# A graph layer whose edge rows go through memory: sends of the next chunk moved ahead of the first fetch, and one block's lists ahead of the first table's stores

## The chip, the cores and the metric

The kernel runs on one core of a Trainium2 chip. The metric is device time in microseconds (us) for one launch, the median of several runs. Engines are named as in the profile: PE (matrix), DVE (vector), ACT (scalar), POOL (GpSimd), SP (the queue from which most plain DMAs leave).

## The reference

```python
h = relu(layernorm(x))                       # x: 12500 x 64
# 212500 edges, sorted by dst; ew: one weight per edge
e = silu(concat(h[row], h[col], ew) @ eW1 + eb1)      # 129 -> 128
e = silu(e @ eW2 + eb2)                               # 128 -> 128
agg = segment_sum(e, row, num_segments=12500)
out = x + silu(concat(h, agg) @ nW1 + nb1) @ nW2 + nb2
```

Here `row` is `src` and `col` is `dst`; the edges come sorted by `dst`.

## The kernel before, in words

The first product is split: A = h @ eW1[:64] is looked up by `src`, B = h @ eW1[64:128] by `dst`. A is kept in memory as table `ta` (three bf16 parts per value), B as table `tb`. Since the edges come sorted by `dst`, the B row of an edge lies in a small window of `tb`; the rows of A and the sums go by `src`, which is in random order. So each edge's partial row is sent through memory to a place that belongs to the bucket of its source (100 buckets of 125 nodes), and read back bucket by bucket.

**Send side.** The edges come in 208 blocks of 1024. For block s:

- `load` reads two lists (`bc`, `bb`: positions in the window and buckets, L265 and L267) for one block further on, and two windows of 48 rows of B for block s itself (L277). All go out from SP's queue. The windows of the first `EARLY` blocks come from a small table `tb0` (the first 2048 nodes) that is ready early; later ones from `tb`.
- `count` makes, on DVE, the selection matrix `pick` (L302), the bucket mask `oh` (L303), its running count (L306) and `own` (L314), and has SP load the edge weights into `pick` (`weights`, L288).
- `send` takes ranks (L333) and the B rows times selection (L341) on PE, copies them to `qs` on ACT (L348, L357), forms addresses `to` on DVE (L353), and sends 128 edges at a time with an indirect DMA from POOL (L362), eight per block. `qs` has eight buffers (of four sends each), `to` four.

A block's sending is cut into `PIECES` = 3 pieces. Blocks are grouped into 11 chunks: 8 blocks in chunk 0, 20 in each later one, each with its own table `q`. `send_all(c)` yields the pieces of a chunk; on its way it also issues the zero fills of the next chunk's `q` (L100, ACT's queue), and it runs the count of one block ahead.

**Receive side.** A batch is four buckets of one chunk, 25 batches in each chunk. `fetch` loads its rows from `q` and its rows of `ta` (L407, L412, both on SP), four batches ahead (`NQ`). A step handles 512 rows: local indices turned (`lr`, L430), one-hot (`oneT`, L435), first layer (`pt`, L444 and L451, activated at L455), second layer (L477, L483, L487), sum by node (L464, L497), added to `aggT` (L506, L508). A batch has one step in chunk 0 and two in later chunks, 525 steps in all. In the last chunk `nodes` follows each batch and writes the output.

**Order.** PE, DVE, ACT and SP run in the order in which the program lists their instructions. The list is written by hand: `turn` gives the order of the parts of neighbouring steps, with four places (`None`, "hooks") per step, at which pieces of the next chunk and parts of `feed` are put in. `feed` is everything that makes `ta`, `tb` and the scaled bucket addresses of the later chunks (`normed`, `products`, `checks`). `marks` gives how many pieces must be out by which hook: all pieces of chunk c by the hook at which the first batch of c is fetched. Between two marks they are spread evenly: 60 pieces in 92 hooks while chunk 0 is received, 60 in 188 or 200 later.

Before the main loop stand the lists: `destinations` and `sources` write the table `rows` (L622, L640), `first_rows` makes `tb0` (stores at L557), then come block 0's scaling and loads, all eight blocks of chunk 0 with four parts of `feed` at each piece, and the first four fetches.

Of the kernel before, what the change touches and what calls it, by code (L numbers as in the profile page):

```python
# [46 lines left out]
G = 4  # L47
# [12 lines left out]
def tile_gnn(ctx: ExitStack, tc: tile.TileContext, x, src, dst, ew, eW1, eb1, eW2, eb2, nW1, nb1, nW2, nb2, out):  # L60
# [18 lines left out]
    chunks = []  # L79
# [25 lines left out]
            dma(to[part], of[part])  # L105

    CH = 12
    NE, EARLY = 16, 24
    x_rows = x.rearrange("(l b) d -> l b d", b=NB)

    ident = const.tile([P, P], F32, name="ident")
# [74 lines left out]
    bkE = const.tile([P, 2 * TB, NP], F32, name="bkE")  # L186
# [4 lines left out]
    for win in wins:  # L191
        nc.vector.memset(win, 0.0)
        for a in range(2):
            for i, row in enumerate((w1d, eb1b)):
                at = a * HB + WL + i
# [43 lines left out]
    with ExitStack() as work:  # L239
# [14 lines left out]
        blk = {}  # L254
        nblocks = -(-E // BLK)
        chunk_of = [c for c, ch in enumerate(chunks) for _ in range(2 * (ch[1] - ch[0]))][:nblocks]

        def load(s, ahead=0):

            if s + ahead < nblocks:  # L260
                p, g = (s + ahead) // 2, (s + ahead) % 2
                r = rows[p, g]
                bc = ld.tile([P, HALF], BF16, name="bc")
                of = bass.AP(tensor=r.tensor, offset=r.offset, ap=[[HALF, 2], [0, HB], [1, HALF]])
                nc.sync.dma_start(bc, of)  # L265
                bb = ld.tile([P, BLK], BF16, name="bb")
                nc.sync.dma_start(bb[:112], bass.AP(tensor=r.tensor, offset=r.offset + BLK, ap=[[0, 112], [1, BLK]]))  # L267
                blk[s + ahead] = [bc, bb]
            if 0 <= s < nblocks:
                p, g = s // 2, s % 2  # L270
                win = wins[s % NW]
                table, end = (tb0, NE * P) if s < EARLY else (tb, N)
                assert s < EARLY or len(done_b) == NB // G
                for a in range(2):
                    h = 2 * g + a
                    at = nc.sync.value_load(base_i[:, h, p : p + 1], min_val=0, max_val=end - WL)
                    nc.sync.dma_start(win[a * HB : a * HB + WL, :], table[bass.ds(at, WL), :])  # L277
                pick = ld.tile([P, HALF], F32, name="pick")
                blk[s] += [win, pick]
# [93 lines left out]
        def send_all(c):  # L373

            mine = [s for s in range(nblocks) if chunk_of[s] == c]
            zeros_left = list(fill(c + 1, nc.scalar, 7)) if c + 1 < len(chunks) else []
            each = -(-len(zeros_left) // len(mine))
            for s in mine:
                load(s + 2, 1)
                for f in zeros_left[:each]:  # L380
                    f()
                del zeros_left[:each]

                for i, _ in enumerate(itertools.zip_longest(count(s + 1), send(s))):
                    pending[c] -= i == PIECES - 1
                    yield
# [4 lines left out]
        PIECES = 1 + TB // G  # L391
        pending = [chunk_of.count(c) for c in range(len(chunks))]
# [125 lines left out]
        hooks = sum(1 for s in turn if s is None)  # L518
# [20 lines left out]
        def turned(xs, g):  # L539

            ht = mm.tile([P, G // 2, P], F32, name="ht", tag="mm")
            for i in range(G // 2):
                nc.tensor.transpose(
                    ht[:, i, :], xs[:, g + 2 * i : g + 2 * i + 2, :].rearrange("p j d -> p (j d)"), ident
                )
            hr = fp.tile([P, G // 2, P], F32, name="hr")
            nc.scalar.copy(hr, ht)
            return hr

        def first_rows(g):  # L550

            hr = turned(x0, g)
            yield
            got = fp.tile([P, G, H], F32, name="got")
            product(1, hr, mm, "mm", got)
            yield
            nc.sync.dma_start(tb0.rearrange("(p j) f -> p j f", j=NE)[:, g : g + G, :], got)  # L557
            yield
# [36 lines left out]
        def turns(todo, width):  # L595

            todo, doing = [x if type(x) is tuple else (None, x) for x in todo], []
            while todo or doing:
                if todo and len(doing) < width and (todo[0][0] is None or todo[0][0] in ready):
                    doing.append(todo.pop(0)[1])  # L600
                for d in list(doing):
                    if next(d, 0) == 0:
                        doing.remove(d)
                    else:
                        yield
# [37 lines left out]
        def by_edges(of, to):  # L643

            for k0 in range(0, 2 * TB, 4):
                tr = mm.tile([P, 4, NP], F32, name="tr", tag="mm")
                for k in range(4):
                    nc.tensor.transpose(tr[:, k, :], of[:, (k0 + k) * P : (k0 + k + 1) * P], ident[:NP, :NP])
                if to is locE:
                    nc.scalar.add(to[:, k0 : k0 + 4, :], tr, 1.0)  # L650
                else:
                    nc.scalar.copy(to[:, k0 : k0 + 4, :], tr)
                yield

        def scale(c):
            p0, p1, cap, _, _ = chunks[c]
            v = bkE[:, :, p0:p1]

            q4 = lp.tile([P, 2 * TB, p1 - p0], F32, name="q4", tag=f"q4{c > 0}")
            nc.vector.tensor_scalar(q4, v, 0.5 - G / 2, 1.0 / G, op0=OP.add, op1=OP.mult)  # L660
            nc.vector.tensor_scalar(q4, q4, float(3 * 2**22), None, op0=OP.add)
            nc.vector.tensor_scalar(q4, q4, -float(3 * 2**22), None, op0=OP.add)
            nc.vector.scalar_tensor_tensor(v, q4, float(cap * P * G - G), v, op0=OP.mult, op1=OP.add)
# [36 lines left out]
        with tc.tile_pool(name="lists", bufs=1, side="right") as lp:  # L700
            x0 = lp.tile([P, NE, D], F32, name="x0")
            nc.sync.dma_start(x0, x[: NE * P, :].rearrange("(p j) d -> p j d", j=NE))
            srcR = lp.tile([NP, PAIR], I32, name="srcR")
            dstR = lp.tile([NP, PAIR], I32, name="dstR")
            f, sf, t = (lp.tile([NP, PAIR], F32, name=n) for n in ("f", "sf", "t"))
            fv = f.rearrange("p (g e) -> p g e", e=HALF)
            lo = lp.tile([NP, 4], F32, name="lo")
            rowsS = lp.tile([NP, 2, 2, BLK], BF16, name="rowsS")
            nc.vector.memset(srcR[96:NP, LAST:], N)
            vec = lambda v, lo_, n, m: bass.AP(tensor=v.tensor, offset=v.offset + lo_, ap=[[m, n], [1, m]])  # L710
            for to, v, queue in ((dstR, dst, nc.scalar), (srcR, src, nc.sync)):
                for p0, p1 in ((0, 96), (96, NP - 1)):
                    queue.dma_start(to[p0:p1, :], vec(v, p0 * PAIR, p1 - p0, PAIR))
                queue.dma_start(to[NP - 1 : NP, :LAST], vec(v, (NP - 1) * PAIR, 1, LAST))
            nc.scalar.dma_start(dstR[NP - 1 : NP, LAST:], vec(dst, E - PAD, 1, PAD))
            zero_fills = list(fill(0, nc.scalar, 7))
            zero_fills.pop(0)()
            steps_ = [norm(x0, NE), destinations(), sources()]
            for _ in turns(steps_, 3):
                if zero_fills:  # L720
                    zero_fills.pop(0)()
            for _ in turns([by_edges(sf, bkE)] + [first_rows(g) for g in range(0, NE, G)], 3):
                pass
            scale(0)
            load(-1, 1)
            load(0, 1)
            load(1, 1)
            for _ in by_edges(t, locE):
                pass
            for _ in count(0):  # L730
                pass
            feed = itertools.chain(checks(), turns(groups(), 3))
            for _ in send_all(0):
                for _ in range(4):
                    next(feed, None)
# [8 lines left out]
            nc.scalar.copy(b2f, p2)  # L744
        ld2 = work.enter_context(tc.tile_pool(name="ld2", bufs=NQ))
        ndp = []
        for i in range(NQ):
            fetch(i)


        first = -3
        marks, total = [(0, 0)], 0
        for c in range(1, len(chunks)):
            start = c * (NB // G) - NQ
            by = sum(x[2] for x in batches[: start + 1]) - 2
            total += PIECES * pending[c]
            marks.append((hooks * (by - first), total))
        pieces = itertools.chain.from_iterable(send_all(c) for c in range(1, len(chunks)))
        at = done = 0
        for k in range(first, len(steps) + 2):  # L760
            for s in turn:
                if s is None:
# [16 lines left out]
                else:  # L779
                    f, ahead = s  # L780
# [8 lines left out]
    with tc.tile_pool(name="fl", bufs=1) as fl, tc.tile_pool(name="flp", bufs=1, space=PSUM) as flp:  # L789
        fp = flp.tile([1, P], F32, name="fp")  # L790
        s = fl.tile([P, 1], F32, name="s")
# [141 lines left out]
```

## Time and profile before

| | us |
|---|---|
| median of 3 runs (2700.62 to 2704.18) | 2703.32 |
| the profiled execution | 2702.45 |
| its span | 2700.7 |
| busy: PE / DVE / ACT / POOL | 2188.2 / 1874.6 / 1251.1 / 1818.5 |
| mean granted PE clock | 0.907 |

Busy times are those of one profiled execution and overlap each other. A group's row in the profile gives its busy time, the mean duration of one instruction in ns, and the idle time of its engine just before it with what ended most of that. A wait is put down to the one event that came last. The issue of a DMA takes its queue's time only for the issue; the transfer runs on without the queue.

### The profile page before, as it was taken

How to read it: one execution, taken by the hardware profiler on the slowest of the kernel's cores; microseconds unless marked ns; L12 is line 12 of the kernel's file. 1: busy time of each engine (PE TensorE's matmuls, PEld its weight loads, DVE VectorE, ACT ScalarE, POOL GpSimd, SP SyncE). 2: the span in 40 equal slices, each digit the busy share in tenths (PEclk: the TensorE clock that was granted, in tenths of full speed). 3: DMA queues.
4: the chain of work that ended last, by engine and by line, in shares of the span. 5: the costliest groups of instructions: out<-in, count | busy, mean ns of one | idle time of the engine just before them, and what ended most of it. 6: DMA issues, size and time to landing. Idle time of an engine off the chain costs nothing.

```text
span 2700.7 us, 59194 instructions
## 1 busy us (share of the span) xinstructions
PE 2188.2 (81%) x21814; PEld 2043.3 (76%) x21814; DVE 1874.6 (69%) x2634; ACT 1251.1 (46%) x2689; POOL 1818.5 (67%) x1728
## 2 busy tenths in 40 slices
PE   2436674898699599699879969959959987997997
PEld 1326574897699599599779869959958986996996
DVE  4736683796588488588768858848857885883443
ACT  2325551454355255355445535525535544553443
POOL 2546787777777777777777777777777777773000
PEclk9757786998899799799989989979989998998999
DMA  8668675876776777686787777767767755764441
GB/s 201 190 186 243 202 246 163 260 234 196 231 234 229 213 248 236 203 251 231 212 256 230 237 218 233 238 205 253 231 202 250 240 183 198 234 199 158 158 164 52
DMA packets 257969, 577.18 MB, mean 214 GB/s; under 512 B 51201, under 2 KB 110579, under 8 KB 257468
## 3 DMA queue, kind: packets, MB, share of 16 engines
q1 hardware_dynamic: 185096, 384.91, 44.3%
q0 software_dynamic: 54144, 123.04, 12.6%
q10 hardware_dynamic: 18434, 65.37, 10.5%
q8 instruction: 175, 2.87, 0.4%
q14 instruction: 120, 0.98, 0.1%
HBM read 361.44 MB, written 211.67 MB: 212 GB/s over the span
## 4 chain that ended last, share of the span: by engine, by line
PE 63%; DMA 13%; issue 6%; POOL 5%; DVE 2%; ACT 1%; SPq 0%; DVEq 0%; POOLq 0%; ACTq 0%
PE p L483 15%; PE seg L497 15%; PE pt L451 11%; DMA q<-qs,to 8%; PE pt L444 8%; PE qp L341 7%; POOL q L362 5%; PE lr L430 4%; DMA pick<-in_edge_weight_dram 3%; PE misc L333 1%; DMA bb<-rows 1%; PE z L216 1%; PE o L225 1%; DVE oneT L435 1%; PE z L219 1%
## 5 line engine op out<-in xcount | busy, mean ns | idle before, releaser
L362 POOL DMA_INDIRECT q<-qs,to x1661 | 1780.4, 1072 | 632.2 <-issue 445.6
L455 ACT ACTIVATE e<-pt 128x512 f32<-128x512 f32 x525 | 313.9, 598 | 778.0 <-PE pt L451 765.1
L483 PE MATMUL p<-w,e 128*128 128x128 f32 x4200 | 588.2, 284 | 2.2 <-ACT p L477 2.2
L497 PE MATMUL seg<-one,e 128*128 128x125 f32 x4200 | 576.8, 281 | 8.9 <-DVE aggT L506 5.7
L483 PEld LDWEIGHTS p<-w,e 128*128 128x128 f32 x4200 | 529.5, 198 | 27.5 <-issue 10.4
L497 PEld LDWEIGHTS seg<-one,e 128*128 128x128 f32 x4200 | 524.8, 196 | 11.2 <-ACT p L477 4.1
L435 DVE TENSOR_SCALAR oneT<-lr,part 125x512 bf16<-125x512 f32 x525 | 392.6, 748 | 197.5 <-PE lr L430 194.6
L306 DVE TENSOR_TENSOR_SCAN run<-oh,run,misc 100x1024 f32<-100x1024 f16 x197 | 461.1, 2341 | 1.0 <-PE misc L333 0.7
L451 PE MATMUL pt<-oneT,a 125*128 125x256 bf16 (+1 forms) x3300 | 444.6, 274 | 0.0
L341 PE MATMUL qp<-win,pick 50*128 50x128 f32 x3322 | 264.6, 300 | 205.0 <-DMA pick<-in_edge_weight_dram 119.9
L348 ACT COPY qs<-qp 128x512 f32<-128x512 f32 x416 | 224.7, 588 | 444.3 <-PE qp L341 312.0
L341 PEld LDWEIGHTS qp<-win,pick 50*128 50x128 f32 x3322 | 224.1, 202 | 237.8 <-issue 208.2
L444 PE MATMUL pt<-ident,qt 128*128 128x128 f32 x2100 | 332.8, 282 | 68.8 <-DVE oneT L435 68.8
L508 DVE TENSOR_TENSOR aggT<-aggT,seg 128x500 f32<-128x500 f32 x250 | 168.3, 673 | 315.7 <-PE seg L497 313.3
L464 DVE TENSOR_TENSOR one<-nodes,qt 128x500 f32<-128x500 f32 x525 | 353.4, 673 | 0.5 <-PE seg L497 0.5
L451 PEld LDWEIGHTS <-a 125*128 125x128 bf16 x3300 | 320.5, 100 | 34.5
L487 ACT ACTIVATE e<-p 128x512 f32<-128x512 f32 x525 | 314.6, 599 | 12.3 <-PE p L483 11.6
L477 ACT COPY p<-b2f 128x512 f32<-128x512 f32 x525 | 312.3, 595 | 0.1
L444 PEld LDWEIGHTS pt<-ident,qt 128*128 128x128 f32 x2100 | 228.4, 145 | 74.9 <-DVE oneT L435 72.9
L430 PE MATMUL lr<-identb,qt 128*125 128x128 bf16 x2100 | 215.1, 226 | 63.1 <-DMA qt<-q 63.0
L314 DVE TENSOR_TENSOR own<-run,oh 100x1024 f16<-100x1024 f32 x208 | 253.7, 1220 | 0.0
L430 PEld LDWEIGHTS <-qt 128*125 128x125 bf16 x2100 | 187.8, 140 | 75.6 <-DMA qt<-q 63.7
(122 smaller groups left out, 1094.5 us busy)
## 6 DMA issues: line engine op xcount, KB each, us to landing
qt<-q SPq DMA_DIRECT2D x250, 576.0 KB
a<-ta SPq DMA_DIRECT2D x275, 384.0 KB
q<-zeros ACTq DMA_DIRECT2D x30, 1638.0 KB
bb<-rows SPq DMA_DIRECT2D x208, 224.0 KB
bc<-rows SPq DMA_DIRECT2D x208, 128.0 KB
q<-qs,to POOLq DMA_INDIRECT x1661
win<-tb SPq DMA_DIRECT2D x416, 24.0 KB
ta<-parts SPq DMA_DIRECT2D x25, 384.0 KB
```

The costliest lines, as they stand in the source:

```text
L306: nc.vector.tensor_tensor_scan(run, oh, nil.to_broadcast([NB, BLK]), carry.get(c, -1.0), op0=OP.add, op1=OP.add)
L341: nc.tensor.matmul(qps[a][:, t, :], pick[half, t * P : (t + 1) * P], win[half, :], start=True, stop=True)
L362: i = nc.gpsimd.indirect_dma_start(out=q[:], out_offset=bass.IndirectOffsetOnAxis(ap=to[:k, t : t + 1], axis=0), in_=qs[:k, t - t0, :], in ...
L430: nc.tensor.matmul(lr[:L, t, :], loc[:, at : at + 1].to_broadcast([P, L]), identb, start=True, stop=True)
L435: nc.vector.tensor_scalar(oneT, st[k].pop("lr")[:L], part1[:L, :], None, op0=OP.is_equal)
L444: nc.tensor.matmul(pt[:, t, :], qt[:, j, :H], ident, is_transpose=True, start=t == 0, stop=False, skip_group_check=True)
L451: nc.tensor.matmul(pt[:, cols, :], a3[:L, b, i, :], oneT[:, cols, :], start=False, stop=i == 2, skip_group_check=True)
L455: nc.scalar.activation(e1, pt, AF.Silu)
L464: nc.vector.tensor_tensor(one.rearrange("p (b j) l -> p b j l", j=n), nodes1[:, None, None, :].to_broadcast(wide), loc[:, tiles[0][1] : ti ...
L483: nc.tensor.matmul(p2[:, t, :], e1[:, t, :], w2, start=False, stop=t == G - 1, skip_group_check=True)
L487: nc.scalar.activation(e2, p2, AF.Silu)
L497: nc.tensor.matmul(item[2][:, b, :], e2[:, t, :], one[:, t, :], start=j < G, stop=j >= G * (n - 1))
```

## The change

There are three edits.

1. `load` is cut in two: `load_rows(s)` loads the two lists of a block, `load(s)` calls it for block s + 1 and then loads the windows of block s. The lists of block 0 are loaded ahead of `first_rows`, and so ahead of the stores of `tb0`, no longer behind them; `scale(0)` is put in among `first_rows`. (`counting = count(0)` makes a generator; its instructions are still listed behind `by_edges(t, locE)`.)
2. `EARLY` goes from 24 to 30: six more blocks take their windows from `tb0`.
3. Nine pieces (`LEAD`: three blocks) of chunk 1 are listed ahead of the first `fetch`, with four parts of `feed` at each. The marks are raised by the same nine for all chunks but the last, so that by the first fetch of a chunk three blocks of the next one have been listed too. For the last chunk there is no next one: 51 pieces are left in its stretch instead of 60.

```diff
-    NE, EARLY = 16, 24
+    NE, EARLY = 16, 30
...
-        def load(s, ahead=0):
+        def load_rows(s):
...
+        def load(s):
+            load_rows(s + 1)
...
-                load(s + 2, 1)
+                load(s + 2)
...
-            for _ in turns([by_edges(sf, bkE)] + [first_rows(g) for g in range(0, NE, G)], 3):
-                pass
-            scale(0)
-            load(-1, 1)
-            load(0, 1)
-            load(1, 1)
+            load_rows(0)
+            counting = count(0)
+            for i, _ in enumerate(turns([by_edges(sf, bkE)] + [first_rows(g) for g in range(0, NE, G)], 3)):
+                if i == 8:
+                    scale(0)
+            for i in range(2):
+                load(i)
             for _ in by_edges(t, locE):
                 pass
-            for _ in count(0):
+            for _ in counting:
                 pass
...
+        pieces = itertools.chain.from_iterable(send_all(c) for c in range(1, len(chunks)))
+        LEAD = 3 * PIECES
+        for done in range(1, LEAD + 1):
+            next(pieces)
+            for _ in range(4):
+                next(feed, None)
         for i in range(NQ):
             fetch(i)
...
-        marks, total = [(0, 0)], 0
+        marks, total = [(0, LEAD)], 0
         for c in range(1, len(chunks)):
             start = c * (NB // G) - NQ
             by = sum(x[2] for x in batches[: start + 1]) - 2
-            total += PIECES * pending[c]
-            marks.append((hooks * (by - first), total))
-        pieces = itertools.chain.from_iterable(send_all(c) for c in range(1, len(chunks)))
-        at = done = 0
+            total += PIECES * chunk_of.count(c)
+            marks.append((hooks * (by - first), total + (LEAD if c + 1 < len(chunks) else 0)))
+        at = 0
```

More of the change, by code (lines that the diff above doesn't have):

```diff
@@ L256, in tile_gnn @@
         chunk_of = [c for c, ch in enumerate(chunks) for _ in range(2 * (ch[1] - ch[0]))][:nblocks]
-        def load(s, ahead=0):
-            if s + ahead < nblocks:
-                p, g = (s + ahead) // 2, (s + ahead) % 2
+        def load_rows(s):
+            if s < nblocks:
+                p, g = s // 2, s % 2
                 r = rows[p, g]
@@ L267, in load @@
                 nc.sync.dma_start(bb[:112], bass.AP(tensor=r.tensor, offset=r.offset + BLK, ap=[[0, 112], [1, BLK]]))
-                blk[s + ahead] = [bc, bb]
-            if 0 <= s < nblocks:
+                blk[s] = [bc, bb]
+        def load(s):
+            load_rows(s + 1)
+            if s < nblocks:
                 p, g = s // 2, s % 2
```

## The prediction

> **What bounds the kernel now.** I read the costliest groups first, then the waits of SP's queue, then the sends cut by stage, then the engines in slices of 20 us. In the groups the row to stop at is POOL's: one indirect DMA ("send") per 128 edges.
>
> ```profile
> L362 POOL DMA_INDIRECT q<-qs,to x1661 | 1780.4, 1072 | 632.2 <-issue 445.6
> L483 PE MATMUL p<-w,e 128*128 128x128 f32 x4200 | 588.2, 284 | 2.2 <-ACT p L477 2.2
> ```
>
> POOL looks only 67% busy, but most of its idle time is "issue": 0.30 us behind nearly every send, waiting for nothing. A send thus holds POOL for 1.27 us at best and 1.37 on average. Here are the sends alone by stage (window, its length, POOL busy, sends, clock, DMA share, GB/s). I cut at the first send of a chunk: chunk 0 in the first row, chunk 1 in the third, chunk 10 in the row before last.
>
> ```profile
> 67.50:176.00 108.50, 71.26 (x64) 0.70 0.65 186
> 176.00:202.00 26.00, 0.00 (x0) 0.50 0.63 197
> 202.00:459.50 257.50, 185.75 (x160) 0.76 0.68 211
> 459.50:691.80 232.30, 175.29 (x160) 0.90 0.72 227
> 691.80:913.70 221.90, 169.13 (x160) 0.94 0.73 230
> 2239.90:2452.50 212.60, 164.19 (x157) 0.95 0.62 203
> 2452.50:2700.70 248.20, 0.00 (x0) 0.96 0.42 140
> ```
>
> Length less busy less 0.303 per send is what POOL truly stood still: 17.8 in the first row, 26.0, 23.3, 8.5, 4.3, 0.8. The six stages not shown (220.0 to 221.7 long) have 2.7 to 4.1, 20.6 in all. Together 101 us between the first send at 67.7 and the last at 2451.3. So **POOL is the bound** from 67.7 on, and the last 248 us are chunk 10's rows, which need the last send. PE and SP show another picture:
>
> ```profile
> SPq L407 <- DVE one L464: 697.8, 221, 6.6
> SPq L407 <- DMA q<-qs,to: 350.2, 11, 34.7
> ```
>
> The first two are SP's waits (in total, times, longest); next, slices of 20 us (length, then busy and count of PE, PEld, DVE, ACT, POOL, clock, DMA share, GB/s).
>
> ```profile
> 800.00:820.00 20.00, 20.00 (x217) 18.95 (x214) 18.13 (x24) 11.64 (x26) 15.43 (x16) 1.00 0.72 225
> 900.00:920.00 20.00, 1.31 (x14) 0.97 (x12) 4.78 (x5) 0.60 (x1) 15.44 (x15) 0.66 0.74 189
> ...
> 640.00:660.00 20.00, 17.02 (x162) 15.92 (x160) 16.38 (x27) 10.25 (x22) 15.50 (x15) 0.91 0.60 196
> ```
>
> Eleven times, once per chunk, SP stands 32 us on average at the fetch L407 until the chunk's sends have landed. Everything behind it in SP's queue stands too, such as edge weights (L288), and PE falls idle for about 20 us (1.31 busy at 900 to 920). But POOL makes 15 to 16 sends in that slice as in any other: it works off its backlog. With the 1980 matmuls of a chunk's stage at 217 in 20 us, PE needs only 182 us per chunk where POOL needs 217 (169 + 160 x 0.303), so PE's stall is mostly spare time. What counts is the POOL gap when the backlog has run dry.
>
> [...] at 882 SP stands for 32.5 us and the next weights leave right after the fetch, at 915.83. [...] sends of 0.97 us while DVE is still (442 to 460) against 1.07 in the mean; the cause is not shown. [...]
>
> **Part 1, lists of block 0.** SP's order becomes bc and bb of block 0, four tb0 stores, then the rest. Nothing is added; 0.60 + 0.47 us of issue move ahead of the stores. The gain is at most these 1 us: block 0's pick at 48.29 comes earlier, but its matmul at 60.69 waits for the weights sent at 55.87, behind windows that need tb0 landed. The loss: bc must wait until the second rows store (issued 28.72) has landed, and the tb0 stores, first at 31.76, stand behind it. Landing isn't shown; bc left unwaited at 41.36, so at most 9.6 us are lost. A tb0 store of that time took 8.5 us (31.76, landed by 40.26), so rows land near 37. I take **+2 us** because POOL's 17.8 us of gaps in chunk 0 absorb some; ends -1 and +10. The earlier scale(0) (four DVE operations of 0.2 us) waits for the same copy of bkE and costs nothing. EARLY 30 only names the smaller table for six more blocks: the same 24 KB window loads, none of which shows a wait on the stores of tb: 0.
>
> **Part 2, nine pieces ahead.** Per block: SP 5 DMAs (two lists, two windows, weights), DVE 4.7 us (0.54 + 0.48 + 2.34 + 1.22 + 0.14), PE 24 matmuls, ACT four copies, 1.7 us, POOL 8 sends. With the three blocks go 36 feed steps and up to three zero fills of 1638 KB on ACT's queue. All are moved, none added.
>
> Price of the move: chunk 0's 24 pieces took from about 58 to 163, 4.4 us each, so nine take 40. The fetch, which SP reached at 163.3 and issued at 180.81, is issued near 203, then without a wait, chunk 0's sends being long landed. The main loop starts 22 us later. Meanwhile POOL, which stood still from 175.6 to 202.15, makes 24 sends at 1.42 (71.26/64 + 0.30): 34 us, to 210.
>
> ```profile
> 174.65 0.97 POOL L362 DMA_INDIRECT q<-qs,to  x1 [0.30 <-issue]
> 180.81 0.32 SPq L407 DMA_DIRECT2D qt<-q  x1
> 191.15 1.47 SPq L562 DMA_DIRECT2D xs<-in_x_dram  x2
> 202.15 0.96 POOL L362 DMA_INDIRECT q<-qs,to  x1 [26.53 <-ACT qs L357]
> ```
>
> After the fetch the first send took 21 us, since the feed's xs load had stood behind SP's wait (191.15) and held DVE and ACT. That cause goes; I expect 10 us, so a hole of some 4 us is late next. Saved: **22 us** (ends 12 and 26).
>
> Chunk 1's 23.3 us of gaps (202 to 345, from feed steps that hold up DVE and ACT) meet a POOL that is better supplied, and a loop with 36 of some 134 feed steps fewer, but up to 5 sends of backlog on entry cover only part: **11 us** saved (0 to 20).
>
> At a boundary, 24 sends of the next chunk now stand between the chunk's last send and the fetch. That a fetch waits for its own chunk alone is seen in the 221 fetches above that waited for a buffer while later sends were open. The backlog is at most 32 sends (8 qs buffers of four), so SP waits for some 8 sends, 11 us, not 32; PE's lead over the fetch hides that, as it hides 12 of 32 us today. The cover of POOL never drains. Of 8.5 + 4.3 + 20.6 = 33 us of gaps I take **21** away (5 to 30), since gaps of about 1 us released by landed sends may stay. PE then waits in small pieces for qs buffers; slice 640 to 660 shows that regime, POOL still at 15 sends. The last boundary keeps its wait: 51 pieces instead of 60 are left for it, and no lead. The 248 us behind it stay.
>
> Sum: 22 + 11 + 21 - 2 = 52. The profiled execution took 2702.45 us (span 2700.7), 0.9 under the median; 2703.3 - 52 = **2651**.
>
> **The rivals.** (a) Only the start gains: the hole of 26 closes in part, and the gaps at boundaries stay, because the fetch still stands as long as now or the one-us waits multiply. For it: gaps there are only 3 to 4 us each. Against: they follow the drained backlog. Saved 12 to 26: 2677 to 2691. This includes the change not doing what it says, a fetch that waits for the lead too. (b) PE's 20 us idle per chunk are returned in full: eleven make 220, 2483. Against: POOL, even with no gap, saves 84 at most behind chunk 0 (26.0 + 23.3 + 33.4 + 0.8), so 2620 is the floor unless sends get shorter. (c) **Slower**: in chunks 2 to 10 PE, now waiting often and briefly, is granted a lower clock and becomes the bound. It decides below 182/218 = 0.83, 218 being my stage after. At 0.81 a chunk takes 225, and nine times 6 to 7 us eat the whole gain; at the 0.76 of chunk 1's stage it takes 240, and nine times 22 on top of my sum give 2849. For it: chunk 1's stage has it. Against: the like regime at 640 to 660 shows 0.91.
>
> **How the numbers follow.** My case 0.62, (a) 0.22, a gain of under 5 us (part 1 at its worst eats (a)) 0.05, (b) 0.03, (c) 0.08. A measurement of this kernel can tell about 0.2%, 5 us. Faster 0.87, same 0.05, slower 0.08. The low end 2615 is POOL without any gap and a few us of shorter sends; the high end 2692 takes in (a), and the unknown costs at their worst.
>
> **What would show it.** Right: in the sends' stages the row without sends is gone, chunks 2 to 9 take 217 to 219; SP's wait for q at L407 falls from 350 to about 150 us; the last 248 us stay. Wrong: first send later than 72; stages of 221 and more; a clock under 0.83 there; a new hole of over 10 us behind the first fetch.

## The result, and the profile after

The kernel after takes **2706.14 us**, the median of 20 runs (2699.44 to 2712.88), beside 2702.74 for 20 runs of the kernel before in the same comparison (2694.84 to 2712.25). The ratio is 1.0012, 95% interval 1.0003 to 1.0022: no change within the 0.2% that count here, and if anything a hair slower. 2651 was forecast. The profiled execution took 2702.3 us, its span 2700.5. One thing is needed to read the experiments: on some chips the kernel before itself takes 3390 to 3450 us, and what ran there is compared only with the kernel before on the same chip.

Line numbers of the kernel after are four higher than before. First the costliest groups of the page; as before, busy time and mean ns of one, then the idle time ahead of it.

```profile
L366 POOL DMA_INDIRECT q<-qs,to x1661 | 1802.3, 1085 | 610.7 <-issue 410.2
L487 PE MATMUL p<-w,e 128*128 128x128 f32 x4200 | 596.5, 287 | 54.6 <-ACT p L481 54.4
```

The idle time ahead of POOL's sends fell from 632.2 to 610.7, as meant. But the same 1661 sends, with the same bytes, cost 1085 ns each where they had cost 1072: 1780.4 went to 1802.3. What was won in idle time (21.5 us) came back as busy time (21.9 us). The next view shows where: the sends by stage (window, length, POOL busy, sends, clock, DMA share, GB/s), cut at the first send of each chunk, from chunk 0 to chunk 4, then chunk 10 and the tail.

```profile
62.50:171.70 109.20, 69.97 (x64) 0.71 0.69 199
171.70:444.30 272.60, 182.74 (x160) 0.73 0.75 228
444.30:669.40 225.10, 176.29 (x160) 0.91 0.68 219
669.40:891.90 222.50, 169.65 (x160) 0.95 0.73 230
891.90:1117.50 225.60, 175.16 (x160) 0.95 0.71 225
...
2239.20:2452.50 213.30, 165.17 (x157) 0.97 0.60 198
2452.50:2700.50 248.00, 0.00 (x0) 0.96 0.43 140
```

The row without sends is gone. Chunk 2 starts at 444.5 instead of 459.7, 15.2 us earlier. From there to the last send the kernel after takes 2008.2 us and the kernel before took 1993.0. Standing still fell from 34 to 23 us there, but POOL's busy time rose from 1523.4 to 1549.6: +26 - 11 = **+15 us, just what the start had won**. That the two cancel to nothing is chance; the experiments below part them. The last send is at 2451.3 in both, and the tail of 248 us is the same.

Now SP's waits at the fetch (in total, times, longest) and, from the waits of all engines, two that rose, first as they were in the kernel before (L353 and L348), then as they are:

```profile
SPq L411 <- DVE one L468: 945.0, 243, 10.3
SPq L411 <- DMA q<-qs,to: 37.7, 4, 32.1
```

```profile
DVE to L353 <- DMA q<-qs,to: 75.6, 17, 7.9
ACT qs L348 <- DMA q<-qs,to: 128.2, 24, 21.1
```

```profile
DVE to L357 <- DMA q<-qs,to: 313.2, 105, 8.6
ACT qs L352 <- DMA q<-qs,to: 284.3, 96, 9.2
```

The long stand at the fetch is gone but for the last boundary (32.1). In its place, DVE and ACT wait about 100 times each, some 3 us, for a landed send to free a `to` or `qs` buffer; before, these were 17 and 24 waits. The slices of 20 us (length, then busy and count of PE, PEld, DVE, ACT, POOL, clock, DMA share, GB/s) show these short waits in place of the stand:

```profile
840.00:860.00 20.00, 17.90 (x188) 16.85 (x188) 15.56 (x24) 9.36 (x20) 15.43 (x16) 1.00 0.79 225
860.00:880.00 20.00, 10.51 (x92) 9.63 (x93) 10.55 (x16) 6.38 (x14) 14.72 (x14) 0.74 0.88 261
880.00:900.00 20.00, 18.50 (x198) 17.46 (x196) 14.58 (x19) 10.09 (x21) 13.69 (x14) 1.00 0.98 272
```

The slice in which PE did almost nothing (1.31 us at 900 to 920) has no counterpart. Yet POOL, whose sends set the end, makes no more of them: 14 to 16 per slice, where it made 15 or 16.

### The profile page after: what moved, and what is told of

It reads as the page before. It is cut to its first block, busy times and chain, and to the rows that moved or that the text cites. A ratio compares the mean times of both kernels' runs of the same rounds, so it can differ in the third digit from the quotient of the medians.

```text
span 2700.5 us, 59228 instructions
## 1 busy us (share of the span) xinstructions
PE 2229.3 (83%) x21814; PEld 2065.8 (76%) x21814; DVE 1873.6 (69%) x2634; ACT 1246.6 (46%) x2687; POOL 1840.3 (68%) x1728
## 4 chain that ended last, share of the span: by engine, by line
PE 37%; DMA 28%; POOL 14%; issue 9%; DVE 6%; ACT 3%; SPq 2%; DVEq 0%; ACTq 0%; POOLq 0%
DMA q<-qs,to 19%; POOL q L366 14%; PE p L487 9%; PE seg L501 9%; PE pt L455 6%; PE pt L448 4%; PE qp L345 4%; DMA pick<-in_edge_weight_dram 3%; PE lr L434 2%; DMA xs<-in_x_dram 2%; DVE own L318 1%; DMA a<-ta 1%; ACT qs L352 1%; DVE oneT L439 1%; PE z L216 1%
## 5 line engine op out<-in xcount | busy, mean ns | idle before, releaser
L366 POOL DMA_INDIRECT q<-qs,to x1661 | 1802.3, 1085 | 610.7 <-issue 410.2
L487 PE MATMUL p<-w,e 128*128 128x128 f32 x4200 | 596.5, 287 | 54.6 <-ACT p L481 54.4
L501 PE MATMUL seg<-one,e 128*128 128x125 f32 x4200 | 586.3, 284 | 43.0 <-DVE aggT L512 31.2
L501 PEld LDWEIGHTS seg<-one,e 128*128 128x128 f32 x4200 | 531.4, 198 | 51.4 <-ACT qs L361 29.4
L352 ACT COPY qs<-qp 128x512 f32<-128x512 f32 x416 | 232.8, 586 | 517.9 <-DMA q<-qs,to 284.3
L310 DVE TENSOR_TENSOR_SCAN run<-oh,run,misc 100x1024 f32<-100x1024 f16 x197 | 461.2, 2341 | 1.8 <-PE misc L337 1.2
L448 PE MATMUL pt<-ident,qt 128*128 128x128 f32 x2100 | 338.3, 286 | 101.2 <-DVE oneT L439 94.7
L468 DVE TENSOR_TENSOR one<-nodes,qt 128x500 f32<-128x500 f32 x525 | 352.8, 672 | 0.5 <-PE seg L501 0.5
L512 DVE TENSOR_TENSOR aggT<-aggT,seg 128x500 f32<-128x500 f32 x250 | 168.0, 672 | 140.5 <-PE seg L501 139.8
L318 DVE TENSOR_TENSOR own<-run,oh 100x1024 f16<-100x1024 f32 x208 | 253.8, 1220 | 0.0
L357 DVE SCALAR_TENSOR_TENSOR to<-misc,bkE 128x8 int32<-128x8 f32 x208 | 32.2, 155 | 313.3 <-DMA q<-qs,to 313.2
```

Source lines behind the costliest of these rows:

```text
L310: nc.vector.tensor_tensor_scan(run, oh, nil.to_broadcast([NB, BLK]), carry.get(c, -1.0), op0=OP.add, op1=OP.add)
L366: i = nc.gpsimd.indirect_dma_start(out=q[:], out_offset=bass.IndirectOffsetOnAxis(ap=to[:k, t : t + 1], axis=0), in_=qs[:k, t - t0, :], in ...
L448: nc.tensor.matmul(pt[:, t, :], qt[:, j, :H], ident, is_transpose=True, start=t == 0, stop=False, skip_group_check=True)
L468: nc.vector.tensor_tensor(one.rearrange("p (b j) l -> p b j l", j=n), nodes1[:, None, None, :].to_broadcast(wide), loc[:, tiles[0][1] : ti ...
L487: nc.tensor.matmul(p2[:, t, :], e1[:, t, :], w2, start=False, stop=t == G - 1, skip_group_check=True)
L501: nc.tensor.matmul(item[2][:, b, :], e2[:, t, :], one[:, t, :], start=j < G, stop=j >= G * (n - 1))
```

## The experiments

**The bookkeeping.** From the timeline I took each send: 0.97 us when nothing disturbs it, 0.303 us of pause behind it. All that a send lasts over 0.97 is called "excess" below; all that POOL stands still beyond the pause is "gaps". First send + 1661 x 0.97 + 1660 x 0.303 + excess + gaps gives the last send within 2 us for every kernel in the table. "In `one`" counts the sends that begin while DVE is working on `one` (L468, which compares node numbers with the fetched rows and reads both from SBUF), with their mean duration. Some 40 to 70 more in each kernel begin up to 0.06 us ahead of `one`; they are called "just ahead" and are not in the column.

| kernel | median us | first send | chunk 2 starts | last send | excess | gaps | in `one`: sends, mean us |
|---|---|---|---|---|---|---|---|
| before | 2702.74 | 67.7 | 459.7 | 2451.3 | 170.6 | 99.8 | 164, 1.169 |
| after | 2706.14 | 62.8 | 444.5 | 2451.3 | 192.4 | 82.8 | 219, 1.247 |
| e17: start alone | 2690.86 | 62.5 | 445.3 | 2436.9 | 157.4 | 103.7 | 172, 1.170 |
| e5: after + PSUM operand | 2653.66 | 63.2 | 436.0 | 2402.5 | 135.5 | 90.5 | 229, 1.005 |
| e6: before + PSUM operand | 2677.10 | 65.6 | 448.5 | 2425.1 | 134.0 | 112.2 | 210, 0.987 |
| e7: after, later fills | 2690.36 | 63.1 | 437.2 | 2439.9 | 190.1 | 73.4 | 199, 1.202 |
| e8: after, eight `to` | 2687.78 | 63.2 | 447.6 | 2438.3 | 184.2 | 77.6 | 209, 1.236 |

The theory that this table came to test: **sends that begin while `one` runs are held up until it ends**, and the new order brings more of them together. Excess in `one` is 164 x (1.169 - 0.97) = 33 us before and 219 x (1.247 - 0.97) = 61 after: +28, beside +22 for the whole excess. Just ahead of it there are 21 us before and 29 after. The rivals: the extra 26 us come from the memory traffic (the DMA share is as high or higher); they come from the waits for buffers, and so from the depth of `to`; or the loss lies in the start, with the boundaries neutral.

A meeting and a near miss, from the timeline of the kernel after (start, duration, engine and line, and in brackets the idle time before it):

```profile
1001.42 0.66 DVE L468 TENSOR_TENSOR one<-nodes,qt 128x500 f32<-128x500 f32 x1
1001.54 1.52 POOL L366 DMA_INDIRECT q<-qs,to  x1 [0.30 <-issue]
1003.37 0.97 POOL L366 DMA_INDIRECT q<-qs,to  x1 [0.30 <-issue]
1003.52 0.67 DVE L468 TENSOR_TENSOR one<-nodes,qt 128x500 f32<-128x500 f32 x1
```

The first send begins 0.12 us after `one` did. `one` ends at 1002.08, and 0.98 us later, at 1003.06, the send ends. In the second pair the send comes first, by 0.15 us, and neither is longer than usual. Over the whole trace the rule is sharper: 144 sends begin between 0.05 us after the start of `one` and 0.17 us before its end, all of them are lengthened, and 118 end 0.83 to 0.85 us after `one` does, as if a send of 0.97 us were stopped 0.13 us after its start. In the kernel before it is 124 of 130. Of the sends just ahead of `one`, 42 of 58 are held as well (30 of 62 before), so the limit lies at a few hundredths of a microsecond ahead and not at the start itself.

**e5 and e6: one operand of `one` from PSUM.** The constant `nodes1` is copied once into PSUM; e5 does it to the kernel after, e6 to the kernel before.

```diff
-        misc = sgp.tile([P, 4 * TB], F32, name="misc")
+        misc = sgp.tile([P, 4 * TB + L], F32, name="misc")
+        nodesP = misc[:, 4 * TB :]
+        nc.vector.tensor_copy(nodesP, nodes1)
...
-                nodes1[:, None, None, :].to_broadcast(wide),
+                nodesP[:, None, None, :].to_broadcast(wide),
```

> The changed kernel with the node numbers that DVE compares in L468 (tile one) read from PSUM instead of SBUF, a copy made once at the start; the same values, the same number of instructions. Theory A (long sends come from DVE instructions with two SBUF inputs, and tile one's share of them grew from 25 to 47 us): no long send beside tile one, total 35 to 50 us less than the changed kernel, 2656 to 2671. Rival (long sends come from the DMA side and only happen to lie beside DVE): no change, 2700 to 2710.

> The kernel before with the same move of the node numbers to PSUM. Theory A: its long sends beside tile one hold 25 us, so 15 to 25 us less, 2678 to 2688, and so less than the changed kernel gains by it; the two are then 15 to 25 us apart, the changed one ahead. Rival: no change, 2703.

Measured: e5 2653.66 us (2644.5 to 2654.81), ratio 0.9812 (0.9789 to 0.9835); e6 2677.1 (2676.01 to 2682.65), ratio 0.9915 (0.9897 to 0.9934). Both gained what theory A said, a little more than its ranges. `one` itself did not get cheaper: first its group in the kernel after, then two groups of e5.

```profile
L468 DVE TENSOR_TENSOR one<-nodes,qt 128x500 f32<-128x500 f32 x525 | 352.8, 672 | 0.5 <-PE seg L501 0.5
```

```profile
L368 POOL DMA_INDIRECT q<-qs,to x1661 | 1745.2, 1051 | 619.9 <-issue 409.2
L470 DVE TENSOR_TENSOR one<-misc,qt 128x500 f32<-128x500 f32 x525 | 351.4, 669 | 2.5 <-PE misc L339 2.0
```

And this is what its timeline shows where a send begins while `one` runs:

```profile
1002.60 0.67 DVE L470 TENSOR_TENSOR one<-misc,qt 128x500 f32<-128x500 f32 x1
1003.13 0.97 POOL L368 DMA_INDIRECT q<-qs,to  x1 [0.30 <-ACT e L461]
...
1029.82 0.67 DVE L470 TENSOR_TENSOR one<-misc,qt 128x500 f32<-128x500 f32 x1
1030.11 0.96 POOL L368 DMA_INDIRECT q<-qs,to  x1 [0.30 <-ACT p L483]
1030.40 1.22 DVE L320 TENSOR_TENSOR own<-run,oh 100x1024 f16<-100x1024 f32 x1
1031.38 1.08 POOL L368 DMA_INDIRECT q<-qs,to  x1 [0.30 <-DMA q<-qs,to]
```

The send at 1030.11 overlaps `one` by 0.38 us and takes 0.96. The next one begins 0.24 us ahead of the end of `own`, which still reads two tensors in SBUF, and takes 1.08. Over the whole run 229 sends begin in `one`, at least as many as in the kernel after, at 1.005 instead of 1.247 us: 61 us of excess became 8, and the 29 us just ahead of `one` went too. Some of it came back elsewhere: sends that begin in `own` have 102 us of excess in e5 and 84 in the kernel after. The whole excess fell by 57. The memory traffic was not touched, so it is not the cause. This shows that the meeting with `one` is what lengthened the sends. Where `one` starts first and has 0.17 us or more to run, the send is held (the 144 sends above, all lengthened). It does not work the other way round: 275 times in the kernel after `one` begins 0.06 to 0.9 us behind a send, and it takes 0.671 us in the mean and 0.677 at most, so the send does not keep it out.

The pair tells a second thing. With excess equal (135.5 and 134.0) e5 is **23 us** faster than e6: 22 in gaps (112.2 to 90.5) and 2 at the first send. That is what the change is worth when `one` no longer holds sends. From chunk 2's start to the last send e5 takes 1966.5 us and e6 1976.6. So the lead at the boundaries, which costs 15 us while `one` reads both operands from SBUF, gains 10 with one of them in PSUM.

**e17: the start alone.** Nine pieces ahead of the first fetch stay; the marks of the later boundaries stand as before.

```diff
-            marks.append((hooks * (by - first), total + (LEAD if c + 1 < len(chunks) else 0)))
+            marks.append((hooks * (by - first), total))
```

> Both parts at the start, no lead at the later boundaries; it parts the start from the boundaries only where the kernel before takes about 2700 us. Theory A (the start gains, the later boundaries lose by longer sends): chunk 2 starts 10 to 20 us earlier than before, later stages as before (220 to 222), total 10 to 18 us less, 2685 to 2693. Theory B (what the start gives is lost in any case): 2703 to 2706. Where the kernel before takes 3400 us: 0.25% to 0.5% less, as in the runs so far.

Measured: 2690.86 us (2686.54 to 2695.39), ratio 0.9956 (0.9941 to 0.9971). SP's long stand at the fetch is back, and the chunks are at their old length:

```profile
SPq L411 <- DMA q<-qs,to: 329.1, 10, 34.7
```

```profile
445.10:680.40 235.30, 175.01 (x160) 0.90 0.71 224
680.40:901.50 221.10, 169.05 (x160) 0.94 0.73 231
901.50:1121.60 220.10, 167.91 (x160) 0.93 0.73 232
```

Chunk 2 starts at 445, as in the kernel after (444.5); from there to the end of the last send e17 takes 1992.9 us (the kernel before 1993.0) and the kernel after 2008.2. This is what theory A said. So the start is worth 12 to 13 us by the medians, and **the lead at the boundaries costs 15**, although it removes the stand that it was meant to remove. The rival that lays the loss in the start is out.

**e7: the zero fills later.** The kernel after lists up to three fills of 1638 KB inside the nine pieces; e7 begins them three blocks later in each chunk.

```diff
-                for f in zeros_left[:each]:
+                for f in zeros_left[: each if c == 0 or s >= mine[0] + 3 else 0]:
```

(and likewise in the `del` below it)

> The changed kernel with the next chunk's zero fills issued from the fourth block of a chunk on, so that the three blocks of the lead carry none. Theory A (the hole behind the lead comes from DMA traffic of the fills that delays the feed's x loads and SP's issues): gaps between 172 and 280 fall from 38 to under 20 us, chunk 2 starts at 425 to 435 instead of 444.5, total 5 to 20 us less. Rival (the hole is the work of the 36 feed steps itself): unchanged start of chunk 2, total 2703 to 2708.

Measured: 2690.36 us (2679.21 to 2695.03), ratio 0.9955 (0.994 to 0.9969). The first fetch leaves at 199.4 instead of 220.88, chunk 1's gaps fall from 41.3 to 31.5, and chunk 2 starts at 437.2, 7 us earlier. That is less than theory A said: chunk 2 was to start by 435, and the gaps between 172 and 280 fall from 37 to 29 us, not to under 20. The last send is 11.4 us earlier in all, so some 4 us come later than the start.

**e8: eight `to` buffers** instead of four (`bufs=4` to `bufs=8` in that pool), so that DVE should no longer be released by landed sends.

> The changed kernel with eight instead of four buffers for the addresses (to), so that DVE no longer waits for landed sends (313 us of waits at L357). Theory A (DVE that is released by landed sends runs in step with POOL, which makes its two-input instructions meet sends more often): long sends beside tile one fall from 47 us towards 25, total 10 to 20 us less. Rival (it is no matter of step): the wait moves to ACT's qs, long sends unchanged, total 2703 to 2708.

Measured: 2687.78 us (2681.49 to 2688.35), ratio 0.9942 (0.9923 to 0.9962). It helps by 18 us by the medians; in the profiled execution the last send is 13 us earlier, 8 by excess and 5 by gaps. The time is that of theory A, the rest is mostly the rival's: DVE's wait for `to` is gone, ACT's for `qs` grew from 284 to 419 us, and sends still begin in `one` 209 times at 1.236 us. Those just ahead of `one` fell from 58 to 39, and their excess from 29 to 14 us. So DVE's wait for `to` is not what brings sends into `one`; it may have part in those just ahead.

**e1 and e9: the lists alone.** Kernel before with `load(-1, 1)` moved ahead of `first_rows` and `scale(0)` put in among them, as in the change; `EARLY` stays at 24 (both runs are of the same kernel).

> Part 1 alone (lists of block 0 ahead of the tb0 stores, EARLY still 24, no lead). Theory A (POOL's sends are one busy chain, a shift of its first send is handed on to the end): first send near 63 instead of 67.7, all stages as before, total 3 to 5 us less, 2698 to 2700. Theory B (a slack later on takes in what the start gives): first send near 63, last send unmoved near 2451, total 2703. The prediction's own step: first send 2 us later, total 2705.

> Part 1 alone again, on a chip where the kernel before takes about 2700 us. Theory A (POOL's sends are one chain): first send near 63, handed on to the end, 2 to 5 us less, 2698 to 2701. Theory B (what the start gives is lost later): 2703. The prediction's own step: first send 2 us later, 2705.

Measured, both on a chip of 3390 to 3450 us: 1.0005 (0.9984 to 1.0027) and 1.001 (0.9981 to 1.0039). The first send is at 62.8 and 63.3, as in the kernel after (62.8): this part alone brings it forward, and `EARLY` has no share in that. `EARLY` was not tested by itself. Whether the gain reaches the end can't be read here, because POOL waits for something else there, as the page of e1 says:

```profile
L362 POOL DMA_INDIRECT q<-qs,to x1661 | 1809.8, 1090 | 1348.7 <-ACT qs L357 726.1
```

**e2 and e3: the two halves of the lead.** e2 is the same kernel as e17; e3 has no lead ahead of the first fetch and raises the marks only from chunk 2's on.

```diff
-        for done in range(1, LEAD + 1):
-            next(pieces)
-            for _ in range(4):
-                next(feed, None)
+        done = 0
...
-        marks, total = [(0, LEAD)], 0
+        marks, total = [(0, 0)], 0
...
-            marks.append((hooks * (by - first), total + (LEAD if c + 1 < len(chunks) else 0)))
+            marks.append((hooks * (by - first), total + (LEAD if 1 < c < len(chunks) - 1 else 0)))
```

> Part 1, EARLY, and the lead of three blocks ahead of the first fetch only; the lead is spent while chunk 0 is received, so later boundaries are as before. Theory A (the lost time of the change lies in chunks 3 to 7, where the sends got longer because DVE no longer stands still at the boundaries): chunk 2 starts 10 to 20 us earlier than before, later stages 220 to 222, total 10 to 18 us less, 2685 to 2693. Theory B (whatever is won at the start is lost in any case): total 2703 to 2706.

> Part 1, EARLY, and the lead at the later boundaries only: nothing of chunk 1 ahead of the first fetch, chunk 1's boundary as before, three blocks ahead from chunk 2's on. Theory A (longer sends at the later boundaries): SP's wait at the fetch gone from chunk 2 on, but stages of 222 to 228, total 2710 to 2725. The prediction's own step (gaps closed, sends unchanged): stages of 218 to 219, total 2680 to 2690.

On such chips e2 gave 0.9946 (0.9921 to 0.997), and its repeats e10, e13, e15 and e16 gave 0.9973, 0.9975, 0.9977 and 0.997, with intervals of 0.002 to 0.003 to either side (e10's reaches 1.0002): a gain of 0.2 to 0.5%, of the size that e17 then measured. e3 gave 1.0005 (0.9983 to 1.0026), and its repeats e11 and e14 0.9951 (0.9921 to 0.9981) and 0.9999 (0.9975 to 1.0023). That the boundaries' lead costs 15 us follows from e17 beside the kernel after; e3, which has that lead without the nine pieces, ran on such chips only and neither shows nor refutes it.

**e4: 104 more sends.** The kernel after with a second send of the last 128 edges of every second block, to a twin table that nobody reads.

> The changed kernel with one send doubled: the last 128 edges of every second block are sent once more, to a table of their own that nobody reads; 104 sends more, 1765 in all, output unchanged. Theory A (POOL's sends set the end): 104 x 1.37 = 142 us more, 2840 to 2855. Rival (POOL only follows; PE, SP or the fetches set the pace): less than 30 us more.

Measured: 1.0351 (1.0305 to 1.0397) on a chip where the kernel before takes 3440.83, some 121 us over the kernel before for 104 sends, where 142 were expected. It fits a chain of sends, but on that chip POOL has other waits too (1348.7 us of idle time ahead of its sends in e1), and nothing here leans on it.

**e12 and e18: all three edits** (e5 + e7 + e8) on the kernel after.

> The changed kernel with all three edits that gained: node numbers in PSUM, zero fills from the fourth block of a chunk on, eight address buffers. Theory A (each takes away its own part of what POOL's chain loses: 45 us of long sends, 10 us of gaps at the start, and of the 18 us of the address buffers only what does not lie in tile one, some 5): 2635 to 2650. Rival (they remove the same time): 2650 to 2660.

> The changed kernel with all three edits that gained: node numbers in PSUM, zero fills from the fourth block of a chunk on, eight address buffers; it counts where the kernel before takes about 2700 us. Theory A (each takes away its own part of what POOL's chain loses: 45 to 50 us of long sends, 10 us of gaps at the start, some 5 by the address buffers): 2635 to 2650. Rival (they remove the same time): 2650 to 2660.

Measured, again on chips of 3390 to 3450 us: 1.0084 (1.0055 to 1.0113) and 1.0208 (1.0153 to 1.0262), slower than the kernel before on the same chip. There PE often stands for nothing that the profile shows; e18's waits have

```profile
PEld qp L347 <- issue: 356.0, 462, 13.0
PE qp L347 <- issue: 253.3, 384, 8.5
```

(208.2 and 82.0 us in the kernel before, in its profile of 2702 us), and POOL waits 689 us for ACT's `qs`, which needs PE. Whether the three edits add up where the kernel takes 2700 us is open; why they lose here is open too, and e5 alone did not run on such a chip. **e5 is the version that is shown to beat both kernels**, by 1.9%, on a chip where the kernel before takes 2701 us.

## Why the prediction was wrong

**The bound was right.** POOL's sends set the end: e6 takes 37 us of excess from them (170.6 to 134.0), gives 12 back in gaps, and the last send comes 26 us earlier; the median falls by 24 (2701.26 to 2677.10, on the same chip). The tail stayed at 248 us, and no gain came from PE's time: PE's stall at the boundary is gone, and that is worth nothing by itself, so rival (b) was rightly low.

**Part 1: +2 us was forecast, 4.9 us were gained** at the first send. That `bc` would wait for the rows was right (6.6 us), and that the stores of `tb0` would go later too (31.76 to 38.62). The failed step is "its matmul at 60.69 waits for the weights". That matmul did not set the first send. The last link was DVE's address operation `to` (66.69 in the kernel before), which stood behind block 1's scan (64.43), whose `pick` had waited for block 1's list. The kernel before:

```profile
42.57 0.55 SPq L265 DMA_DIRECT2D bc<-rows  x1
55.68 0.55 DVE L302 TENSOR_SCALAR pick<-bc,same,plus 128x512 f32<-128x512 bf16 x1 [2.61 <-DMA bc<-rows]
64.43 2.34 DVE L306 TENSOR_TENSOR_SCAN run<-oh,run,misc 100x1024 f32<-100x1024 f16 x1
66.69 0.14 DVE L353 SCALAR_TENSOR_TENSOR to<-misc,bkE 128x8 int32<-128x8 f32 x1
67.70 1.12 POOL L362 DMA_INDIRECT q<-qs,to  x1 [28.10 <-issue]
```

Now:

```profile
35.86 0.57 SPq L265 DMA_DIRECT2D bc<-rows  x1
38.62 4.79 SPq L561 DMA_DIRECT2D tb<-got  x4
43.46 0.56 SPq L265 DMA_DIRECT2D bc<-rows  x1
49.95 0.55 DVE L306 TENSOR_SCALAR pick<-bc,same,plus 128x512 f32<-128x512 bf16 x1 [4.21 <-DMA bc<-rows]
58.68 2.34 DVE L310 TENSOR_TENSOR_SCAN run<-oh,run,misc 100x1024 f32<-100x1024 f16 x1
60.94 0.14 DVE L357 SCALAR_TENSOR_TENSOR to<-misc,bkE 128x8 int32<-128x8 f32 x1
62.84 1.06 POOL L366 DMA_INDIRECT q<-qs,to  x1 [23.57 <-ACT qs L361]
```

Block 1's `pick` is now at 49.95, before it was at 55.68; the scan follows it by 8.7 us in both kernels, and the first send follows the scan by 4.2 us (3.3 before), now released by ACT's `qs`. The list that this `pick` waits for is not the one that was moved: block 1's list went out 0.9 us later than before (43.46, 42.57 before), but `pick` began 6.5 us after that issue instead of 13.1 (the issue itself takes SP 0.56 us, 0.55 before). Every trace with the lists moved has 6.2 to 6.5, the two without 13.1 and 13.4 (e6). In the kernel before, a zero fill had gone out just ahead of that list (42.38); in the kernel after it follows (44.52). Whether that made the list late is not shown.

**The nine pieces: 33 us were forecast for the hole and chunk 1's gaps, 8 came.** The hole of 26 and the 23.3 us of gaps behind it became 41.3 us in several pieces:

```profile
209.03 1.82 SPq L566 DMA_DIRECT2D xs<-in_x_dram  x2
216.54 0.95 DVE L528 TENSOR_REDUCE mean<-xs 128x12 f32<-128x768 f32 x1 [13.17 <-DMA xs<-in_x_dram]
219.97 1.29 POOL L366 DMA_INDIRECT q<-qs,to  x1 [11.68 <-DVE own L318]
220.88 1.84 SPq L411 DMA_DIRECT2D qt<-q  x1
```

A load of `feed` went out at 209, DVE waited 13.17 us for it, and the next block's `own` and so POOL stood behind DVE for 11.68. It is the very wait that the prediction saw behind the old fetch ("the feed's xs load had stood behind SP's wait"); "that cause goes" was wrong, since it moved along with the 36 steps of `feed`. The step "nine take 40" was too small as well: the fetch left at 220.88, not near 203. e7 names the reason: with the fills out of the nine pieces it leaves at 199.4 and 10 us of gaps go. The prediction had counted the fills as moved and priced them at nothing.

**The boundaries: 21 us were forecast, -15 came.** SP's wait fell further than forecast, from 350 to 37.7 us and not to 150; of the 34 us of gaps in chunks 2 to 10, 11 went, half of the 21. The step that failed is the one that was not argued: chunk stages of "169 + 160 x 0.303", with the 169 taken from the old stages. The sends did not stay as long as they were: in chunks 2 to 10 they took 1549.6 us instead of 1523.4, and this +26 outweighs the gaps. The prediction had noted the sends of 0.97 us beside a still DVE, against 1.07 in the mean; it even said "unless sends get shorter". It did not ask what a boundary without stall does to them.

In the old boundary PE stood, and with it DVE (4.78 us busy of 20 at 900 to 920), while POOL worked off its backlog undisturbed. That stall was cover. The trace of the kernel before has ten stretches of 19 to 30 us in which DVE does nothing; 152 sends of chunks 2 to 10 begin in them, and they take 0.97 us each. In the kernel after, 47 sends are left in stretches of 8 us or more, 11 of them at the last boundary. The other sends of the kernel before have 0.101 us of excess each; at that rate the 105 that lost their cover cost 11 us, an estimate from these two numbers. The rest of the 26 us is a higher rate, 0.112 in the kernel after, where 55 more sends begin in `one`. That meetings with `one` cost this time is shown (e5, e6); why their number rises from 164 to 219, and in e6 also to 210 although its fetch still stands, stays open. One hint: if all sends of chunks 2 to 10 are shifted against `one` by 1.5 to 6 us, either way, some 223 begin in it in the mean, in either kernel (62 to 409, according to the shift); in truth it is 157 in the kernel before and 212 in the one after. So the two engines run in step, and the old order met `one` less often than shifted ones do in the mean.

**The rivals.** (a), only the start gains, gave 2677 to 2691; that is what e17 measures (2690.86), without the boundaries' loss. (c), slower by a lower clock, was wrong in its cause: the clock in chunks 2 to 10 is 0.91 to 0.97, no lower than before (0.90 to 0.95 in the stages shown). The mechanism that decided was in no rival.

**The sum.** Forecast 22 + 11 + 21 - 2 = 52. Measured, by the last send: 4.9 for part 1, 5.9 in gaps and 4.5 in excess up to chunk 2, then -15.2: 0.

## What to carry to other kernels

Price a chain of sends from POOL as their number times the undisturbed send and pause, plus the time lost by sends that begin while DVE runs an operation that holds them (in the kernel after 61 us in `one` and 84 in `own`; which operations hold sends is read from the trace); the mean send duration of a profile holds such meetings, and a new order changes their number. An idle stretch of the other engines may be cover for the bound engine (here for 152 sends, at 0.97 us each): before removing it, ask what the bound engine does meanwhile and what it will meet instead. Where the meeting can't be avoided, try one operand in PSUM: for `one` that made 24 us without the change (2701.26 to 2677.10) and some 50 with it (2706.14 to 2653.66, on chips whose kernels before are 1.5 us apart).

## What the runs showed of the hardware

- A send that begins while `one` runs is held: in the kernel after 118 of 144 such sends end 0.83 to 0.85 us after `one` does. A send that begins 0.06 to 0.9 us ahead of `one` is not (0.967 us in the median), and it does not lengthen `one` (0.671 us in the mean); of the 58 that begin less than 0.06 us ahead, 42 are held. A DVE operation on the same shapes with one operand in PSUM takes as long (669 ns, 672 before) and does not hold sends (1.005 us, beside 1.247; none of 72 just ahead).
- `own` (L318, 1.22 us, both inputs in SBUF) does the same at a higher price: 88 sends of the kernel before begin in it and take 1.80 us in the mean; in e5 195 do, at 1.49. That is the largest part of the excess that remains. To move one of its inputs was not tried.
- e5's theory A spoke of two SBUF inputs; that is too narrow. In the kernel after `pick` (L306) and `oh` (L307), which compare one list each with constants, hold sends too: 57 begin in `pick` and take 1.18 us in the mean, 29 begin in `oh` and take 1.22. Sends that begin in the scan (L310, 2.34 us long) are not held (311, 0.967 us in the mean, 0.972 at most), nor are those in `aggT` (L512; 106, 0.967 and 0.979); both operations have one input in PSUM. What parts the two kinds was tested for `one` alone.
- The same program takes 2703 us on one chip and 3390 to 3450 on others. e1, which differs from it only in the place of one block's lists and scaling, took 3452.74 us there in its profiled execution, at a granted clock of 0.835; that of the kernel before took 2702.45 at 0.907. The cause is not known.
